# Moving the conditions' set-up of a fused MoE, linear-attention and local-attention kernel

## The chip, the cores and the metric

The kernel runs on one core of a Trainium2 chip. The metric is the device time of one execution in microseconds (us), here the median of three runs. One more execution was recorded by the hardware profiler; all times inside the kernel are from that one, counted from the start of its span. All data are 32-bit floats.

## The reference

The input `x` is 4 batches of 512 rows of 256 numbers, with a condition of 64 numbers for each batch. Three parts follow each other:

```
x = x + linear_attention(mixture_of_experts(x, cond))
x = x + ffn_and_local_attention(conditioned_attention(x, cond))
```

The mixture has 8 experts of three layers (256 to 512 to 512 to 256) and takes two of them for each row. The linear attention has 8 heads in blocks of 32 rows. The conditioned attention has 16 heads, and mixes its softmax with a "field" over the positions that depends on the condition alone. That field is what this case is about:

```
fp = layernorm(relu(cond @ We1.T + be1) @ We2.T + be2, ln_g, ln_b)   # 4 x 256
fa = softmax(fp @ pe.T)                                               # 4 x 512, pe: sines of the positions
mod = (1 - 0.21) * mod + 0.21 * fa                                    # in the conditioned attention
```

The condition also gives a bias to the conditioned attention's coherence (`cond` times a part of `Wc1`, plus `bc1`). Last come two layers of a local attention with a gated feed-forward.

## The kernel before

**Experts.** The rows are sorted by expert into slots of 256 or 128 rows. `SLOTS` lists 24 of them; the last two (`rare`) run only if the routing needs them, under a run-time branch (`tc.If`, L1508). For each of the others (`often`), the loop at L1487 does the first layer (`layer`, matmuls into `ph`, then the activations `h`, by turns on ACT and DVE), then the third layer of the slot before (`last`: matmuls into `po`, a bias addition on DVE into `ob`, L1464, and one indirect DMA of 128 rows on POOL's queue into the table `ys` in DRAM, L1469, one or two of them), then the second layer. The last of these slots has 128 rows, the one before it 256. The scatters all write `ys`, and each waits until the one before has landed. In iterations 2 and later one weight of the later stages is loaded each (`later`), so the weights of the conditions are there some iterations before the loop ends.

**The conditions' set-up.** `conditions` (L229) is a generator of small operations on 4 or 8 columns, with two `yield`s, so three parts:

- first: `pcs` (the condition times two weights), `csb` and `hdT` on DVE, `pfp`, and the layer norm of `fp` on DVE, with a square root on ACT (L250);
- second: two transposes of `fp` (`pfpT`), a copy, `pfs` (the product with the positions, 512 wide), and a copy of it into `fa` (L264);
- third: maximum `fmx` (L267), Exp with its sum `fsum` on ACT (L269), scaling, four transposes (`pfaT`) and a copy into `faT`.

Before, the first part stands behind the loop and ahead of the branch, the second behind the branch, and the third is chained into the linear attention's work for the first batch (`fill`, L1681), from which pieces are taken between the steps of the attention. `faT` and `csb` are used in the conditioned attention, more than 100 us later.

**Filling.** `busy(n)` (L1390) puts n matmuls 512 wide whose result nobody reads (`pbusy`) into PE's queue. It reads batch 0's `xres`, so POOL's addition to it (L1557) waits for the last of them.

**Results.** `results(b)` (L1521) loads batch b's two rows of `ys` for each row into `g0` and `g1`, two buffers of each; batch 0's in halves, the second row's on ACT's queue, all others on SP's. `weighted(b)` (L1532) scales them on ACT (`g`, L1535) and adds on DVE (`ymoe`, L1536). Batches 2 and 3 get the buffers of batches 0 and 1. The linear attention's `front` then transposes `ymoe` (`pt`), copies it (`yT`), and multiplies (`pqk`, `pv`); `features` does `pf` and, on ACT, `ex`.

**What sets the order.** A planner puts the instructions of each engine into its queue: of those that it takes to be ready, the one earliest in the program goes first. So work can run ahead of its place in the program, or behind it. Instructions pinned to program order (those under `PE.in_order()`, `busy` and the whole linear attention on PE among them) keep behind whatever the program issued before them on the engine. The matmuls of the experts' layers and of `conditions` are not pinned where it is called from the experts' stage. On the chip each queue runs in order.

The calls around the branch, before:

```
            last(len(often) - 1, often[-1])
            aside = conditions(cw_, wp)
            next(aside)
            busy(1)
            with tc.If(halves > NHALF - NRARE):
                ...
            busy(3)
            next(aside)
            busy(1)
```

Of the kernel before, what the change touches and what calls it, by code (L numbers as in the profile page):

```python
# [12 lines left out]
F32 = mybir.dt.float32  # L13
I32 = mybir.dt.int32
AF = mybir.ActivationFunctionType
ALU = mybir.AluOpType
AX = mybir.AxisListType
PSUM = bass.MemoryType.PSUM

B, S, H = 4, 512, 256  # L20
# [43 lines left out]
def adaln_attn_ffn_kernel(ctx: ExitStack, tc: tile.TileContext, a: dict, out: bass.AP):  # L64
    nc = tc.nc
# [40 lines left out]
    def bank(kind, name):  # L106
        return ps_now["pool"].tile([128, 512], F32, tag=kind, name=name, bufs=ps_now[kind])

    def mmt(name):
        return bank("mm", name)  # L110

    def tpt(name):
        return bank("tp" if "tp" in ps_now else "mm", name)

    def acct(name):
        return bank("acc" if "acc" in ps_now else "mm", name)
# [10 lines left out]
    def mm(dst, pairs):  # L127
        for i, (lhsT, rhs) in enumerate(pairs):
            PE.matmul(dst, lhsT, rhs, start=(i == 0), stop=(i == len(pairs) - 1))
# [11 lines left out]
    def run(pieces):  # L141
        for _ in pieces:
            pass
# [22 lines left out]
    def col(name, i=0):  # L166
        at = COLS[name][0] + i
        return cols[:, at : at + 1]
# [11 lines left out]
    def row(name):  # L180
        return rows[name]
# [49 lines left out]
    def conditions(W, cp):  # L231

        csb = cp.tile([128, 2, B], F32, tag="csb", name="csb", bufs=1)
        hdT = cp.tile([128, 2, B], F32, tag="hdT", name="hdT", bufs=1)
        for c in range(2):
            ps = acct("pcs")
            PE.matmul(ps[:, 0:B], W["wc1c"][:, c * 128 : (c + 1) * 128], W["csT"], start=True, stop=True)
            PE.matmul(ps[:, B : 2 * B], W["we1"][:, c * 128 : (c + 1) * 128], W["csT"], start=True, stop=True)
            nc.vector.tensor_scalar(csb[:, c, :], ps[:, 0:B], col("bc1", c), None, ALU.add)
            nc.vector.tensor_scalar(hdT[:, c, :], ps[:, B : 2 * B], col("be1", c), 0.0, ALU.add, ALU.max)  # L240
        ps = acct("pfp")
        mm(ps[:B, :H], [(hdT[:, c, :], W["we2"][:, c, :]) for c in range(2)])
        fp = cp.tile([B, H], F32, tag="fp", name="fp", bufs=1)
        nc.vector.tensor_tensor(fp, ps[:B, :H], row("be2")[:B, :], ALU.add)
        st = cp.tile([B, 6], F32, tag="fst", name="fst", bufs=1)
        nc.vector.bn_stats(st, fp)
        mv = cp.tile([B, 2], F32, tag="fmv", name="fmv", bufs=1)
        nc.vector.bn_aggr(mv, st)
        rs = cp.tile([B, 1], F32, tag="frs", name="frs", bufs=1)
        nc.scalar.activation(rs, mv[:, 1:2], AF.Sqrt, bias=eps5[:B, :])  # L250
        nc.vector.reciprocal(rs, rs)
        nc.vector.tensor_scalar(fp, fp, mv[:, 0:1], rs, ALU.subtract, ALU.mult)
        nc.vector.tensor_tensor(fp, fp, row("lng")[:B, :], ALU.mult)
        nc.vector.tensor_tensor(fp, fp, row("lnb")[:B, :], ALU.add)
        yield
        pt = tpt("pfpT")
        for c in range(2):
            PE.transpose(pt[:, c * B : (c + 1) * B], fp[:, c * 128 : (c + 1) * 128], ident[:B, :B])
        fpT = cp.tile([128, 2, B], F32, tag="fpT", name="fpT", bufs=1)
        nc.vector.tensor_copy(fpT, pt[:, : 2 * B].rearrange("p (c b) -> p c b", b=B))  # L260
        ps = mmt("pfs")
        mm(ps[:B, :], [(fpT[:, c, :], W["peT"][:, c, :]) for c in range(2)])
        fa = cp.tile([B, S], F32, tag="fa", name="fa", bufs=1)
        nc.vector.tensor_copy(fa, ps[:B, :])  # L264
        yield
        fmx = cp.tile([B, 1], F32, tag="fmx", name="fmx", bufs=1)
        nc.vector.reduce_max(fmx, fa, axis=AX.X, negate=True)  # L267
        fsum = cp.tile([B, 1], F32, tag="fsum", name="fsum", bufs=1)
        nc.scalar.activation(fa, fa, AF.Exp, bias=fmx, accum_out=fsum)  # L269
        nc.vector.reciprocal(fsum, fsum)  # L270
        nc.vector.tensor_scalar(fa, fa, fsum, FIELD, ALU.mult, ALU.mult)
        pt = tpt("pfaT")
        for t in range(NT):
            PE.transpose(pt[:, t * B : (t + 1) * B], fa[:, t * 128 : (t + 1) * 128], ident[:B, :B])
        faT = cp.tile([128, NT, B], F32, tag="faT", name="faT", bufs=1)
        nc.vector.tensor_copy(faT, pt[:, : NT * B].rearrange("p (t b) -> p t b", b=B))
        W["csb"], W["faT"] = csb, faT
# [865 lines left out]
    with ExitStack() as abc:  # L1143
        wp = abc.enter_context(tc.tile_pool(name="wp", bufs=1, reuse_waits="tile"))
# [6 lines left out]
        with ExitStack() as moe:  # L1151
# [35 lines left out]
            with PE.in_order():  # L1187
# [7 lines left out]
                for n, b in enumerate((0, 2, 3, 1)):  # L1195
# [6 lines left out]
                    for t in range(NT):  # L1202
                        nc.scalar.activation(sq[:, t, :], xres[b][:, t, :], AF.Square,
                                             accum_out=ss[:, b * NT + t : b * NT + t + 1])
# [45 lines left out]
            rest = xp.tile(G, F32, tag="rest", name="rest")  # L1250
# [139 lines left out]
            def busy(n):  # L1390
                with PE.in_order():
                    ps = mmt("pbusy")
                    for _ in range(n):
                        PE.matmul(ps, ident, xres[0].rearrange("p t h -> p (t h)")[:, :512], start=True, stop=True)
# [86 lines left out]
            cw_ = {}  # L1481
# [3 lines left out]
            gather(0, ds[0])  # L1485
            often, rare = ds[:-NRARE], range(len(ds) - NRARE, len(ds))
            for j, d in enumerate(often):  # L1487
                if j == len(often) - 2:
                    halves = nc.values_load(nhalf[0:1, 0:1], min_val=0, max_val=2 * NE)
                if j == 1:  # L1490
                    weights()
                h1 = layer(d, d.xbT, "h1", d.w1[:, 8:].rearrange("p (c m) -> p c m", m=ME), 0)
                if j:
                    last(j - 1, ds[j - 1])
                if j + 1 < len(often):
                    loads(j + 1, ds[j + 1])
                    gather(j + 1, ds[j + 1])
                    if j > 1 and later:
                        name, behind[0] = next(iter(later)), True
                        cw_[name] = later.pop(name)()  # L1500
                        behind[0] = False
                d.h2 = layer(d, h1, "h2", d.w2, 4)
            last(len(often) - 1, often[-1])

            aside = conditions(cw_, wp)
            next(aside)
            busy(1)
            with tc.If(halves > NHALF - NRARE):  # L1508
                for j in rare:
# [3 lines left out]
                    h1 = layer(d, d.xbT, "h1", d.w1[:, 8:].rearrange("p (c m) -> p c m", m=ME), 0)  # L1513
                    d.h2 = layer(d, h1, "h2", d.w2, 4)
                    last(j, d)
            busy(3)
            next(aside)
            busy(1)


            def results(b):  # L1521
# [21 lines left out]
        with ExitStack() as lin:  # L1543
# [111 lines left out]
            def beside(b):  # L1655
                if b + 1 < B:
                    nxt = front(b + 1, ds[b + 1])
                else:
                    nxt = cond_front(cw_, 0, cond_first, False, v1s, wp, gp, {"xT2": "g0", "cT": "g1"})
                for _ in range(6):  # L1660
                    next(nxt, None)
                    yield
                if b > 0:
                    yield from tail(b - 1, ds[b - 1])
                yield from nxt

            with PE.in_order():


                rest = front(0, ds[0])  # L1670
                for _ in range(4):
                    next(rest)
                features(ds[0], 0)
                for _ in range(2):
                    next(rest)
                fill = iter(())
                for k in range(len(steps) + 1):
                    b, u = steps[k] if k < len(steps) else (B, 0)
                    if u == 0:
                        run(fill)  # L1680
                        fill = (beside(b) if b else chain(rest, aside, beside(0))) if b < B else iter(())  # L1681
                    if b < B:
                        ds[b].fm_now = ds[b].fm
                    if u % 2 == 0 and k > 0:
                        b0, u0 = steps[k - 1]
                        values(ds[b0], u0 // 2)
                        next(fill, None)
                    if k + 1 < len(steps):
                        b1, u1 = steps[k + 1]
                        features(ds[b1], u1)  # L1690
                    next(fill, None)
                    if b < B:
                        scores(ds[b], u)
                    next(fill, None)
                run(fill)
# [3 lines left out]
        with ExitStack() as cst:  # L1699
# [3 lines left out]
            cp = cst.enter_context(tc.tile_pool(name="cp", bufs=2, reuse_waits="tile"))  # L1703
# [10 lines left out]
    with ExitStack() as again:  # L1714
        again.enter_context(banks("ps3", mm=4, tp=2, acc=2))
        with tc.If(wrong > 0):
            with ExitStack() as cst:
                wp = cst.enter_context(tc.tile_pool(name="wp2", bufs=1))
                cp = cst.enter_context(tc.tile_pool(name="cp2", bufs=2))
# [130 lines left out]
```

## Time and profile before

| what | value |
|---|---|
| median of three runs | 1389.45 us (1389.37 to 1392.45) |
| profiled execution, its time | 1390.6 us |
| profiled execution, its span | 1388.8 us |
| mean granted clock of TensorE | 0.988 |
| PE busy | 1336.5 us (96%), 7624 matmuls |
| DVE busy | 655.3 us (47%) |
| ACT busy | 587.2 us (42%) |
| POOL busy | 233.2 us (17%) |
| PE's share of the chain that ended last | 88% |

The span runs from the first to the last instruction; the execution's own time has 1.8 us more. PE is TensorE's matmul row, PEld its weight loads, DVE the vector engine, ACT the scalar engine, POOL GpSimd, SP the engine that issues most DMAs. A float32 matmul shows as two rows of each. The granted clock is the share of full speed at which TensorE was let run in a stretch. The releaser of a wait is inferred from semaphore events.

### The profile page before, as it was taken

The page shows a single profiled execution, that of the slowest core. Times are in us where ns is not written, and L with a number is a line of the kernel's source. Part 1 is how long each engine was busy: PE and PEld are TensorE (multiplying, and loading weights), DVE is VectorE, ACT ScalarE, POOL GpSimd, SP SyncE. Part 2 cuts the span into 40 slices and gives each one's busy share as a digit, 9 for nine tenths or more (in the row PEclk, how much of TensorE's full clock was granted, in tenths as well). Part 3 has the DMA queues.
Part 4 walks back from the last instruction along what each step waited for, and adds up shares of the span by engine and source line. Part 5 has one row for each costly group of instructions (what it writes and reads, how often), then busy time and mean ns, then how long its engine had stood idle before and what let it go on. Part 6 is the DMA issues. An engine that isn't in the chain of part 4 may idle for free.

```text
span 1388.8 us, 19451 instructions
## 1 busy us (share of the span) xinstructions
PE 1336.5 (96%) x7624; PEld 828.0 (60%) x7624; DVE 655.3 (47%) x1296; ACT 587.2 (42%) x997; POOL 233.2 (17%) x223
## 2 busy tenths in 40 slices
PE   5999999998999999999999999999999999999998
PEld 4788888883666633333335555656655556556654
DVE  6122222225777633332227697654362767864421
ACT  4111111115555355454655746662223657474111
POOL 1324322211000011010103232100020322310110
PEclk8999999999999999999999999999999999999999
DMA  4577667633000000000201001210001010011000
GB/s 142 208 255 261 234 217 251 203 131 125 1 2 1 1 0 1 1 1 1 88 30 43 17 25 32 77 41 24 23 0 42 24 33 24 17 40 40 23 24 25
DMA packets 43085, 94.74 MB, mean 68 GB/s; under 512 B 9568, under 2 KB 25064, under 8 KB 40168
## 3 DMA queue, kind: packets, MB, share of 16 engines
q1 hardware_dynamic: 37560, 81.81, 17.7%
q0 software_dynamic: 3792, 10.24, 2.2%
q8 instruction: 63, 1.03, 0.3%
q10 hardware_dynamic: 1632, 1.34, 0.3%
q14 instruction: 38, 0.31, 0.1%
HBM read 84.08 MB, written 7.21 MB: 66 GB/s over the span
## 4 chain that ended last, share of the span: by engine, by line
PE 88%; DVE 6%; ACT 2%; DMA 2%; issue 1%; POOLq 0%; POOL 0%; DVEq 0%; SPq 0%; ACTq 0%
PE ph L78 14%; PE pdq L78 12%; PE pfy L78 6%; PE pug L78 5%; PE pv L78 5%; PE pua L78 5%; PE sc L78 5%; PE po L78 4%; PE pn L78 4%; PE pdy L78 4%; PE pds L78 4%; PE pz L78 2%; PE pqt L82 2%; PE pcy L78 1%; PE pck L78 1%
## 5 line engine op out<-in xcount | busy, mean ns | idle before, releaser
L78 PE MATMUL pdq<-wqkv,yT 128*128 128x512 f32 x384 | 177.1, 602 | 0.0
L419 ACT ACTIVATE cex<-sc 128x1024 f32<-128x1024 f32 x128 | 124.0, 1021 | 99.7 <-PE sc L78 99.0
L78 PE MATMUL ph<-h,w 128*128 128x256 f32 (+1 forms) x704 | 132.9, 346 | 0.4 <-DVE h L1403 0.4
L627 POOL TENSOR_TENSOR qr<-t,t 128x512 f32<-128x512 f32 x64 | 85.9, 1342 | 266.5 <-DVE t L624 229.3
L671 DVE TENSOR_TENSOR p<-p,lmask 128x384 f32<-128x384 f32 (+1 forms) x128 | 92.2, 734 | 69.4 <-ACT p L669 68.2
L78 PEld LDWEIGHTS ph<-h,w 128*128 128x128 f32 x704 | 116.2, 191 | 12.6 <-DVE h L1403 0.8
L78 PEld LDWEIGHTS pdq<-wqkv,yT 128*128 128x128 f32 x384 | 69.6, 190 | 78.1 <-issue 72.8
L1401 ACT ACTIVATE h<-ph,w 128x256 f32<-128x256 f32 (+1 forms) x88 | 35.3, 437 | 190.1 <-PE ph L78 132.2
L1403 DVE TENSOR_SCALAR h<-ph,w 128x256 f32<-128x256 f32 (+1 forms) x88 | 36.1, 438 | 165.7 <-PE ph L78 102.1
L669 ACT ACTIVATE p<-pds,ss 128x256 f32<-128x256 f32 (+1 forms) x256 | 95.8, 456 | 38.8 <-PE pds L78 30.3
L78 PE MATMUL pug<-hT,w 128*128 128x512 f32 x160 | 76.8, 602 | 0.0
L78 PE MATMUL sc<-qm,kT 32*128 32x512 f32 x512 | 76.2, 647 | 0.3 <-ACT cex L419 0.3
L78 PE MATMUL pua<-hT,w 128*128 128x512 f32 x160 | 75.2, 592 | 0.0
L617 ACT ACTIVATE sq<-pdq 128x512 f32<-128x512 f32 x64 | 38.3, 598 | 85.8 <-PE pdq L78 48.1
L78 PE MATMUL pv<-cex,v 128*32 128x512 f32 x512 | 69.1, 605 | 3.6 <-DVE xT L293 2.1
L78 PE MATMUL ph<-xbT,w 128*128 128x256 f32 (+1 forms) x352 | 69.1, 349 | 0.5 <-ACT xbT L123 0.5
L390 POOL TENSOR_SCALAR fterm<-vw,faT 128x256 f32<-128x256 f32 x16 | 14.6, 921 | 323.4 <-DVE cr L380 323.4
L78 PE MATMUL po<-w,h 128*128 128x256 f32 x296 | 67.6, 379 | 0.5 <-ACT h L1401 0.5
L78 PE MATMUL pds<-qT,kT 64*128 64x256 f32 (+1 forms) x512 | 65.3, 375 | 0.0
L78 PEld LDWEIGHTS pds<-qT,kT 64*128 64x128 f32 x512 | 43.9, 186 | 32.9 <-issue 24.7
L78 PEld LDWEIGHTS ph<-xbT,w 128*128 128x128 f32 x352 | 59.2, 193 | 6.8 <-ACT xbT L123 0.7
L78 PE MATMUL pdy<-wo,oT 128*128 128x256 f32 x256 | 61.5, 386 | 0.0
(302 smaller groups left out, 2131.5 us busy)
## 6 DMA issues: line engine op xcount, KB each, us to landing
w<-in_moe_w_dram SPq DMA_DIRECT2D x22, 1024.0 KB
w<-in_moe_w_dram SPq DMA_DIRECT2D x22, 640.0 KB
w<-in_moe_w_dram SPq DMA_DIRECT2D x22, 516.0 KB
zb<-rows SPq DMA_DIRECT2D x32, 256.0 KB
g<-ys SPq DMA_DIRECT2D x6, 512.0 KB
wqkv<-in_f_wqkv_dram SPq DMA_DIRECT2D x2, 1536.0 KB
w<-in_f_w_dram SPq DMA_DIRECT2D x2, 1408.0 KB
out_dram<-yc SPq DMA_DIRECT2D x16, 128.0 KB
```

Of the source, the lines that this page charges most:

```text
L78: cls._queue(nc.tensor.matmul(*args, **kw))
L82: cls._queue(nc.tensor.transpose(*args, **kw))
L390: nc.gpsimd.tensor_scalar_mul(fterm[:, t, :], vw, W["faT"][:, t, b : b + 1])
L419: nc.scalar.activation(ex, pss[j], AF.Exp, scale=CHD**-0.5)
L617: nc.scalar.activation(sq, p3, AF.Square)
L627: nc.gpsimd.tensor_tensor(qr_t[:, s], t1, t2, ALU.add)
L669: nc.scalar.activation(p[:, at], pss[r][:, at], AF.Exp, scale=d.ss[:, 2 * u + jj, 1, 2 * c + r : 2 * c + r + 1])
L671: nc.vector.tensor_tensor(p[:, :n], p[:, :n], lmask[:, :n], ALU.mult)
L1401: nc.scalar.activation(dst, src, AF.Relu, bias=bias)
L1403: nc.vector.tensor_scalar(dst, src, bias, 0.0, ALU.add, ALU.max)
```

## The change

The first part of `conditions` is called at the head of the loop's last iteration, ahead of that slot's first layer. The second part is called behind the loop, ahead of the branch; the copy of `pfs` into `fa` is dropped, and the maximum and Exp read `pfs` in PSUM. The third part is split by a new place of the second `yield`: maximum, Exp and scaling come directly behind the branch, then `busy(4)`, then the transposes and `faT`, then `busy(2)`. Before it was `busy(3)`, the second part, `busy(1)`. The chain into the linear attention no longer holds a part of it.

```diff
@@ conditions
         ps = mmt("pfs")
         mm(ps[:B, :], [(fpT[:, c, :], W["peT"][:, c, :]) for c in range(2)])
-        fa = cp.tile([B, S], F32, tag="fa", name="fa", bufs=1)
-        nc.vector.tensor_copy(fa, ps[:B, :])
         yield
         fmx = cp.tile([B, 1], F32, tag="fmx", name="fmx", bufs=1)
-        nc.vector.reduce_max(fmx, fa, axis=AX.X, negate=True)
+        nc.vector.reduce_max(fmx, ps[:B, :], axis=AX.X, negate=True)
+        fa = cp.tile([B, S], F32, tag="fa", name="fa", bufs=1)
         fsum = cp.tile([B, 1], F32, tag="fsum", name="fsum", bufs=1)
-        nc.scalar.activation(fa, fa, AF.Exp, bias=fmx, accum_out=fsum)
+        nc.scalar.activation(fa, ps[:B, :], AF.Exp, bias=fmx, accum_out=fsum)
         nc.vector.reciprocal(fsum, fsum)
         nc.vector.tensor_scalar(fa, fa, fsum, FIELD, ALU.mult, ALU.mult)
+        yield
         pt = tpt("pfaT")
@@ the experts' loop
             for j, d in enumerate(often):
+                if j == len(often) - 1:
+                    aside = conditions(cw_, wp)
+                    next(aside)
                 if j == len(often) - 2:
@@ behind the loop
             last(len(often) - 1, often[-1])
-            aside = conditions(cw_, wp)
             next(aside)
             busy(1)
             with tc.If(halves > NHALF - NRARE):
...
-            busy(3)
             next(aside)
-            busy(1)
+            busy(4)
+            run(aside)
+            busy(2)
@@ the linear attention
-                        fill = (beside(b) if b else chain(rest, aside, beside(0))) if b < B else iter(())
+                        fill = (beside(b) if b else chain(rest, beside(0))) if b < B else iter(())
```

## The prediction

> **What bounds the kernel now.** The page first: PE is busy for 96% of the span and carries 88% of the chain that ended last. So the change, which touches some 45 us out of 1388.8, is worth what it takes from or adds to the start of the dense PE work behind it. I then read the chain of waits from 250 us on (before 304 us it is matmuls alone), the instructions in order of time from 296 to 358 us, and stretches with the granted clock.
>
> The chain of waits, in order of time (start, us, what):
> ```profile
> 304.51 0.70 DVE ob L1464
> ...
> 305.48 3.84 DMA ys<-ob,goal
> ...
> 309.58 2.53 DMA ys<-ob,goal
> ...
> 312.86 3.15 DMA ys<-ob,goal
> ...
> 316.07 3.18 DMA g<-ys
> ...
> 320.52 3.46 PE pfs L78 x4
> 323.98 1.07 PE pbusy L78 x2
> ...
> 328.99 3.82 DMA g<-ys
> ...
> 332.89 0.91 ACT g L1535 x2
> ```
> Between experts and attention PE waits for transfers. The last-but-one slot's result (`ob`, 304.51) starts three scatters, each held until the one before has landed: 305.48, 309.58, 312.86, all landed at 316.0. Batch 0's rows are then loaded and weighted; its last `ymoe` ends at 322.04 (two of 0.44 from 321.16). PE is not free then: it does `pfs` and a `pbusy`, and the first transposes of the attention (`pt`) start at 325.09, 3.05 late. Further on, batch 3's loads start when batch 1's last `ymoe` ends (328.96) and land at 332.81, with ACT waiting for them ahead of the features.
>
> Instructions in order of time (start, us, engine, line; in brackets the idle time before and its releaser):
> ```profile
> 308.56 1.99 PE L78 MATMUL po<-w,h 128*128 128x256 f32 x8 [0.52 <-ACT h L1401]
> 311.60 1.11 PE L78 MATMUL pfp<-cwe,hdT 128*4 128x256 f32 x4
> 315.04 2.81 PE L78 MATMUL pbusy<-xres,ident 128*128 128x512 f32 x6 [1.27 <-DVEq L1508]
> 316.62 1.28 ACT L250 ACT_TABLE_LOAD   x1 [7.33 <-DMA ys<-ob,goal]
> 325.09 1.09 PE L82 MATMUL pt<-ident,ymoe 128*128 128x128 f32 x8
> 326.43 1.28 ACT L269 ACT_TABLE_LOAD   x1
> ```
> The Sqrt of the set-up comes before the branch in the program, yet ran behind ACT's wait for the scatters. Queue order is thus the planner's, and it can differ from the program's.
>
> Stretches (length, then busy us of PE, PEld, DVE, ACT, POOL, granted clock, DMA share, GB/s):
> ```profile
> 295.00:300.00 5.00, 5.00 (x29) 4.51 (x28) 0.73 (x2) 0.84 (x2) 0.97 (x1) 1.00 0.35 140
> 320.50:324.00 3.50, 3.48 (x5) 0.46 (x5) 1.15 (x3) 2.34 (x6) 0.00 (x0) 0.54 0.98 336
> 342.00:346.00 4.00, 4.00 (x22) 3.51 (x22) 1.90 (x3) 1.57 (x2) 0.00 (x0) 0.72 0.00 0
> ```
> PE has no free time among the experts, and `pfs` ran at about half clock.
>
> **First part, moved ahead of the last slot's first layer.** Its weights were there long before 310 us and no gap took its matmuls, so I put them where the program now has them: behind the last-but-one slot's second layer (about 299.0), ahead of `po` of that slot. Eight `pcs` matmuls take 1.05 (310.48 to 311.60 less the wait of 0.09), four `pfp` 1.04 (311.60 to 312.64). PE is full, so `po`, `ob` and the first scatter move by 2.1: 305.48 becomes 307.6. The scatters keep their spacing (4.10, 3.28, 3.14) and all have landed at 318.1. Bounds: nothing, if PE finds a gap such as the 0.52 at 308 or the matmuls come behind `po`; 2.5, if PE also waits for `hdT`, where its weight load stood 0.42. I take 2.1.
>
> DVE's share is 1.85 up to the variance, 1.37 behind the root (0.15, 0.40, 0.41, 0.41); ACT's is 1.28 table load and 0.29. From 301 on the chain ends near 306.2, before `ob` is due at 306.6. Queued behind the Sqrt on ACT are the last slot's first-layer `h`. They must be done when PE ends `po` (306.5); the Sqrt ends near 304.7, and the four take 1.6. Free, then, with 0.2 in hand; an overrun reaches only the third scatter, which has 1.9 of room (`ob` of the last slot would be ready at 313.1, its turn is 315.0).
>
> **Second part, directly behind the experts.** `pfpT` 0.25, copy 0.16, `pfs` four at 0.43 at full clock (as `pbusy`, six in 2.81) instead of 3.46. About 312.7 to 315.2, wholly inside the wait for the scatters, so nothing on the path. `busy(1)` ends near 316.0; the branch then takes what it took, 1.27, and `busy(4)` runs to about 320.7.
>
> **Third part.** The copy of `fa` (0.68) goes. The maximum now reads PSUM: 0.67 from SBUF, 0.69 for a 512-wide PSUM copy, so no change. Exp needs its table: 1.28 + 0.72 + 0.19. I put it behind ACT's two load issues, where the Sqrt was: 318.9 to 321.1. Batch 0's rows land at 321.3 (3.18 after their issue), so the weighting on ACT is not held, by 0.2. The last transposes (0.7) and `busy(2)` (0.86 each) follow until about 324.0.
>
> A rule that speaks against this: the Trainium skill (ScalarE: Activation LUTs, What ACT_TABLE_LOAD costs) puts a switch of table set at some 2.66 us, a load of 1283 ns and a drain as long again. Here Sqrt starts at 317.92, 0.02 behind its load's end: the load agrees, the drain is not there. By the page Exp would end at 322.5 and the sum below would be +0.6; by the row it is what follows.
>
> **The sum.** `pt` now waits for `ymoe` alone: 322.04 + 2.1 = 324.14 instead of 325.09, a gain of 0.95. But everything that hangs on the loads is 2.1 later. Batch 1's data, there at about 323.6 (some 2.1 MB moved by then, at 336 to 354 GB/s in the stretches), come at 325.7. Its four `ymoe` (0.47 each) no longer queue behind the copy and the maximum, but one of them still meets POOL's `xres` addition (one took 1.73 instead of 0.47). They end between 327.6 and 329.0; I take 328.4, against 328.96. Batch 3's loads and ACT's chain behind them come 0.6 earlier. That is the later bound, so it decides: -0.6. Four transposes (0.7) leave PE at 348.4, but there the chain goes from `pf` to ACT's `ex` at 349.05, which they do not hold: nothing, bound -0.7. The profiled execution took 1390.6 (span 1388.8 and 1.8 around it), which gives 1390.0. Its time is 1.15 above the median of the runs, so in their terms 1389.45 - 0.6 = 1388.8. By the bounds (first part 0 to 2.5, `ymoe` 327.6 to 329.0, transposes, the clock at 342) the forecast's own range is -3.2 to +2.
>
> **Rivals.** *ACT's queue comes free as well.* If the first part's matmuls cost PE nothing ahead of `po` (-2.1) and the planner no longer puts batch 3's weighting ahead of the features, whose wait at 332.89 was 2.22, the gain is 0.6 + 2.1 + 2.2 = 4.9: 1384.5. For it: DVE and ACT lose some 2 us each of work in 324 to 330. Against it: PE is 5.00 busy in each 5 us from 250 to 305.
>
> *The softmax ahead of ACT's loads* (slower). If Exp comes first in ACT's queue, it waits for the maximum (about 318.0) and ends at 318.9, and ACT's half of batch 0's loads starts 0.8 late, behind SP's batch 1 (1 MB, 3 us at 353 GB/s). Batch 0 is weighted up to 3 later, `pt` starts at 327.1, and batch 3's loads land at 334.4, +1.6. PE would then stand for 3 us. Before, a gap of 2.0 (317.85 to 319.87) was followed by 0.54; a cold run costs some 1.9 (the first `pv` 3.61, the second 1.73), so up to +3.5, and with the wait of 0.4 for `hdT` +3.9: 1393.3. It decides from an Exp that starts later than 317.2. For it: program order. Against it: where the Sqrt ran.
>
> The Trainium skill (TensorE: Matmul & The Clock Gate, What's actually happening) has the half clock after an idle window of about 3.4 us. The trace shows it after 2.0, so the shorter gap decides here.
>
> *No effect:* the 3 us that PE gets back are paid by the scatters' 2.1 and the loads; it is the forecast's upper half.
>
> **How the numbers follow.** Forecast 0.52, free queue 0.25, softmax ahead of the loads 0.18, other orders of the replanned queues 0.05 (either sign; an extra wait of 1.2 in each of the four batches of about 35.5 us would be +4.8). A measurement of this kernel tells about 0.3%, 4.2 us, from no change. Faster by more: most of the free queue and the forecast's lowest end, 0.27. Slower by more: the upper half of the softmax case, with a stall on ACT or another order on top, 0.2. Same 0.53. The range takes the free queue's 1384.5 with a little more gain and the softmax case's upper end: 1384.2 to 1393.6.
>
> **What would show it.** Right: `pcs` near 299; first scatter near 307.6, the last landed near 318.1; `pfs` in about 1.9 at clock 1.0 before the branch; Exp behind ACT's loads; `pt` near 324.1; batch 3's loads landing near 332.2. Wrong: the first scatter still at 305.5, Exp ahead of the loads, a half clock over `pt` and `pqk`, or `g` of batch 3 elsewhere on ACT.

## The result, and the profile after

The changed kernel took 1386.4 us (median of 9 runs, 1382.35 to 1387.08), the kernel before 1389.53 beside it (9 runs): a ratio of 0.997, 95% interval 0.9959 to 0.998. In a second series, the run `again` below, it was 1383.66 against 1387.28, ratio 0.9977 (0.9968 to 0.9986). Every ratio in this document is to the kernel before, run beside it in the same series. So the change saves 3 to 4 us, about 0.3%, where the forecast was 0.6. The profiled execution of after took 1386.8, span 1385.0, against 1390.6 and 1388.8 before: 3.8 less.

The chain of waits of the changed kernel (start, us, what), for the lines shown of before:

```profile
310.75 1.02 PE pfs L78 x2
311.78 1.94 PE po L78 x8
313.74 0.44 DVE ob L1464
...
314.44 3.15 DMA ys<-ob,goal
...
318.09 4.42 DMA g<-ys
...
323.08 1.97 DVE ymoe L1539 x2
...
326.43 5.36 PE pqk L78 x8
...
333.81 0.50 ACT g L1538
334.31 0.94 ACT ex L1599
...
339.94 1.92 PE pv L78 x8
```

The long `pfs` with its `pbusy` ahead of the attention (320.52 before) is gone from the chain; half of `pfs` is now on it further up, ahead of the last slot's `po`. Batch 3's loads (328.99 before) are gone too: behind `pqk` the chain goes on with the features, and ACT's `g` of batch 3 (333.81) stands between two `ex` with no wait for data.

Instructions of the changed kernel in order of time (start, us, engine, line; in brackets the idle time before and its releaser):

```profile
301.81 1.03 PE L78 MATMUL pfp<-cwe,hdT 128*4 128x256 f32 x4
...
304.52 1.28 ACT L250 ACT_TABLE_LOAD   x1
...
315.40 0.68 ACT L268 ACTIVATE fa<-pfs,fmx 4x512 f32<-4x512 f32 x1 [2.57 <-DVE fmx L265]
...
322.31 2.34 POOL L1560 TENSOR_TENSOR xres<-xres,crows 128x1024 f32<-128x1024 f32 x1 [5.20 <-DMA g<-ys]
...
323.08 2.25 DVE L1539 SCALAR_TENSOR_TENSOR ymoe<-g,m,g 128x256 f32<-128x256 f32 x2 [0.55 <-ACT g L1538]
...
324.99 1.16 PE L82 MATMUL pt<-ident,ymoe 128*128 128x128 f32 x6 [2.16 <-DVE ymoe L1539]
...
332.89 1.02 ACT L1598 ACTIVATE ex<-pf 128x1024 f32<-128x1024 f32 x1 [1.00 <-PE pf L78]
...
333.81 0.50 ACT L1538 ACTIVATE g<-g,m 128x256 f32<-128x256 f32 x1
```

The first part lies among the last slot's matmuls, and Exp (315.40) lies ahead of the loads, not behind them. POOL's addition to `xres` now runs beside batch 0's last two `ymoe`: 2.25 for the two, against 0.88 for the same two before (321.16). ACT's `g` of batch 3 (333.81) comes behind the first `ex`, where before two of them came ahead of it and had waited 2.22 for their loads.

Stretches of the changed kernel (length, then busy us of PE, PEld, DVE, ACT, POOL, granted clock, DMA share, GB/s):

```profile
312.50:315.50 3.00, 3.00 (x10) 1.11 (x8) 1.10 (x2) 0.43 (x2) 0.97 (x1) 1.00 0.03 5
...
326.00:330.00 4.00, 3.72 (x7) 1.60 (x6) 2.27 (x5) 1.29 (x3) 0.00 (x0) 0.57 0.83 263
...
480.00:484.00 4.00, 4.00 (x64) 3.07 (x66) 2.05 (x6) 0.05 (x1) 1.93 (x3) 0.58 0.00 0
```

and one of the kernel before:

```profile
490.00:494.00 4.00, 3.93 (x20) 1.39 (x20) 0.01 (x1) 0.93 (x2) 2.29 (x3) 0.62 0.00 0
```

`pfs` runs at full clock now. But half clock stands elsewhere: over `pqk` at 326 and over the matmuls at 480 in after; over the first `pv` at 342 and over the conditioned attention at 490 in before.

To see where the time went, both traces are counted from the same place, the transposes `pxb` of the last slot's input rows (291.94 before, 291.85 after), which stand ahead of everything that was moved. All times in the experiments below that are called "from pxb" are counted so. Some names of the linear attention's later steps are needed: `psc` are the score matmuls behind the features, `pn` and `pz` the numerator and denominator in PSUM, `z` the reciprocal of the denominator, and `aT` their product on DVE.

| event, us from pxb | before | after | difference |
|---|---|---|---|
| first scatter of the last-but-one slot | 13.54 | 15.87 | +2.33 |
| batch 0's loads issued | 24.13 | 25.80 | +1.67 |
| first `pt` | 33.15 | 30.25 | -2.90 |
| last `pt` done | 34.24 | 34.30 | +0.06 |
| first `pqk` (its 8 took 3.70, 5.36) | 34.53 | 34.58 | +0.05 |
| first `ex` | 41.76 | 41.04 | -0.72 |
| first `pv` (3.68, 1.99) | 48.82 | 48.03 | -0.79 |
| first `psc` | 52.33 | 49.86 | -2.47 |
| reciprocal `z` at the linear stage's end | 194.10 | 193.26 | -0.84 |
| first `pv` of the conditioned attention | 198.13 | 195.71 | -2.42 |
| end of the span | 1096.86 | 1093.15 | -3.71 |

The clock's part behind the start of `pqk` can be taken out, as an estimate. Half clock cost before 1.69 (`pv`, 3.68 instead of 1.99) and 1.42 (from the conditioned attention's first `pv` to its second 4.07 instead of 2.65), together 3.11; after 1.66 (`pqk`, 5.36 instead of 3.70) and 1.63 (`psc` to `z`: the whole difference between the kernels there is put down to the half clock at 480), together 3.29. So the clock gave nothing there (+0.18), and the work is 3.89 shorter: 2.44 up to `psc` (2.47 + 1.66 - 1.69), by that count nothing from there to `z`, 1.58 from `z` to the conditioned `pv`, and 0.13 back later. The half clock over `pfs` (3.46 before, for two times 1.02 after) lies ahead of `pqk`, and nothing of it is left there: `pqk` starts at the same time in both. The experiments ask for the cause of the 2.44 and the 1.58, and for what became of the 0.95 that PE was to gain and the 2.1 that it was to pay.

### The profile page after: what moved, and what is told of

It reads as the page before. It is cut to its first block, busy times and chain, and to the rows that moved or that the text cites. A ratio compares the mean times of both kernels' runs of the same rounds, so it can differ in the third digit from the quotient of the medians.

```text
span 1385.0 us, 19458 instructions
## 1 busy us (share of the span) xinstructions
PE 1338.2 (97%) x7628; PEld 829.6 (60%) x7628; DVE 655.0 (47%) x1295; ACT 587.7 (42%) x997; POOL 232.7 (17%) x223
## 4 chain that ended last, share of the span: by engine, by line
PE 89%; DVE 5%; ACT 2%; DMA 1%; issue 1%; SPq 0%; POOLq 0%; POOL 0%; DVEq 0%
PE ph L78 14%; PE pdq L78 12%; PE pfy L78 6%; PE pug L78 5%; PE pv L78 5%; PE pua L78 5%; PE sc L78 5%; PE po L78 5%; PE pn L78 4%; PE pdy L78 4%; PE pds L78 4%; PE pz L78 2%; PE pqt L82 2%; PE pqk L78 1%; PE pcy L78 1%
## 5 line engine op out<-in xcount | busy, mean ns | idle before, releaser
L390 POOL TENSOR_SCALAR fterm<-vw,faT 128x256 f32<-128x256 f32 x16 | 14.6, 925 | 323.0 <-DVE cr L380 323.0
L78 PEld LDWEIGHTS pds<-qT,kT 64*128 64x128 f32 x512 | 43.9, 186 | 32.9 <-issue 25.0
```

The lines of the kernel that those rows point to most:

```text
L78: cls._queue(nc.tensor.matmul(*args, **kw))
L390: nc.gpsimd.tensor_scalar_mul(fterm[:, t, :], vw, W["faT"][:, t, b : b + 1])
```

## The experiments

**The 1.58 at the linear stage's end.** Before, the conditioned attention's first `pv` waits for the last `aT`:

```profile
490.07 1.08 PE L78 MATMUL pv<-cex,v 128*32 128x512 f32 x8 [1.50 <-DVE aT L1633]
```

and after it does not:

```profile
487.56 1.07 PE L78 MATMUL pv<-cex,v 128*32 128x512 f32 x8
```

That `pv` reads nothing of `aT`. But `aT` reads `pn` in PSUM, and a new tile in the bank of `pn` has to wait for it. The third part's `pfaT` took a bank of the linear stage's four before, and takes none there after. The theory: this moves `pn` to another bank. The rival: it is the matmuls that left. `again` is the changed kernel once more; `bank1` gives back one bank with four tiny transposes in `pfaT`'s old place, `bank4` takes four banks with sixteen:

```diff
+            def spare():
+                for _ in range(1):          # bank4: range(4)
+                    pt = tpt("pspare")
+                    for t in range(NT):
+                        PE.transpose(pt[:, t * B : (t + 1) * B], ident[:B, :], ident[:B, :B])
+                return
+                yield
-... chain(rest, beside(0)) ...
+... chain(rest, spare(), beside(0)) ...
```

> The changed kernel once more, as the base of the other runs on this chip. Both theories: 3 to 4 us below the kernel before (ratio 0.997). The start of the linear attention and the place of the half-clock stretches are looked at: if the 1.7 us that the first pv gained (1.92 instead of 3.61) is the clock's phase, it can be gone in this profile; if it follows from the order of the work, pv takes about 1.9 again and pqk about 5.4.

> The changed kernel with four 4-column transposes of the identity into one bank of their own, whose result nobody reads, at the place in the linear attention where pfaT was. Theory A (the later half of the gain is that pfaT no longer takes one of the linear attention's four PSUM banks, so the banks come in another order at the end of the stage): the first pv of the conditioned attention waits for aT again, about 1.5 us, and the time is 1.2 to 1.8 us above the changed kernel (ratio to the kernel before about 0.998). Theory B (PE's work that left the stage, 0.4 to 0.7 us of transposes): at most 0.7 us above the changed kernel, seen at 346 to 350 us, and no wait of pv for aT.

> The same with four banks and sixteen transposes, four times the work, but four banks are a whole turn. Theory A: no wait of the first pv for aT, the time within 0.7 us of the changed kernel (ratio about 0.9975). Theory B: four times the loss of the run with one bank, 1.6 to 2.8 us above the changed kernel.

Measured: `again` 1383.66, ratio 0.9977 (0.9968 to 0.9986); `bank1` 1386.16, 0.9989 (0.998 to 0.9999); `bank4` 1383.12, 0.9971 (0.9957 to 0.9985). From `z` to the first `pv`: 2.45, 4.03, 2.44. In `bank1` the wait is back, to the hundredth:

```profile
484.56 1.06 PE L78 MATMUL pv<-cex,v 128*32 128x512 f32 x8 [1.50 <-DVE aT L1636]
```

`bank4`, with four times the extra matmuls, has none. So it is the bank. One caution: the profiled spans of `bank1` and `again` are equal (1380.5 and 1380.9), as the execution of `again` had half clock at 323 to 326 and at 538 to 541 and that of `bank1` nowhere between 280 and 700. The medians are 2.5 apart, but the intervals of the two ratios overlap, so it is the traces that decide here.

From the other side, the same with three spare banks was tried in the kernel before, so that with `pfaT` four are taken:

```diff
-... chain(rest, aside, beside(0)) ...
+... chain(rest, aside, spare(), beside(0)) ...     # spare with range(3)
```

> The kernel before with 12 transposes of 128x4 more (about 0.7 us of PE in all), into three spare banks behind pfaT in the linear stage. With pfaT's own that makes four, a full turn of the four banks, so the banks stand at the stage's end as in the changed kernel. Theory (the turn of the banks is what the 1.58 us at the linear stage's end come from): the conditioned attention's first pv no longer waits for the last aT; from the reciprocal z to pv 2.45 instead of 4.03; 1 to 1.6 us less in all, ratio 0.9985 to 0.9995. Rival (it needs the changed set-up): pv still waits 1.50, ratio 1.0 to 1.001.

1387.74, ratio 1.0 (0.9992 to 1.0009), and the wait of 1.50 is still there. The expectation failed, and the banks in the built programs show why: they fit a rule by which a tile gets the bank that was given back first, not the next in a fixed turn. The tile behind the stage's first ten gets bank 6 in every kernel: `pfaT` before, `pt` after. In `bank4` the four spares, which nobody reads, take 6, 5, 4, 7 and give them back in that order, so `pt` has 6 as in after. In `before_bank3` they take 5, 4 and 7 behind `pfaT`, but `pfaT`'s own bank is given back later, by the copy that reads it, and `pt` gets 5 as before. So no bank behind them moved, and nothing was tested but this.

What can be read off each program is the bank itself. The conditioned `pv` is in bank 6 everywhere. The last `pn` is in bank 6 in before, `bank1`, `before_bank3`, `before_gpin` and `before_gpin3`, and all five wait 1.50 or 1.51; it is in bank 7 in after and in the eight other kernels, and none of them waits. That settles the place; only the count of four is dropped.

**The 0.95 of PE.** `busy` reads `xres`, so POOL's addition waits for the last `pbusy`. If that is why the last `ymoe` were slow, `busy` off another tile should free them:

```diff
+            warm = [xres[0].rearrange("p t h -> p (t h)")[:, :512]]
             def busy(n):
...
-                        PE.matmul(ps, ident, xres[0].rearrange("p t h -> p (t h)")[:, :512], start=True, stop=True)
+                        PE.matmul(ps, ident, warm[0], start=True, stop=True)
...
+            warm[0] = cw_["peT"][:, 0, :]
             next(aside)
```

> The changed kernel with the filling matmuls behind the experts reading the positions' table instead of batch 0's xres, so that POOL's addition to xres need not wait for the last of them. If that addition, which ran at 322.3 to 324.7 beside batch 0's ymoe, is what ate PE's gain: ymoe of batch 0 takes 4 x 0.47 without a stall, its last one ends near 323.7 instead of 325.4, pt and pqk come 1.4 to 1.7 us earlier, PE stands less and keeps its clock; 1.5 to 3 us below the changed kernel (ratio about 0.9955). Rival (the loads set the pace there): ymoe's end and pqk move by less than 0.4, and the time does not change.

1383.28, ratio 0.997 (0.9959 to 0.9981). The two `ymoe` took 0.88, and `pt` was done 32.56 from pxb instead of 34.30. So the collision with POOL is what ate the gain at `pt`. The time that was expected of it, 1.5 to 3 us, did not come: `again` took 1383.66 on the same chip. `pqk` started at 34.17, only 0.41 sooner:

```profile
324.40 3.70 PE L78 MATMUL pqk<-yT,awqkv 128*128 128x512 f32 x8 [1.61 <-ACT yT L123]
```

ACT's half of the copy `yT` stood behind three weightings of batch 1 that waited for their loads. The next step takes that copy off ACT:

```diff
-                    evac(yT[:, c, :], pt)
+                    (evac if b else nc.vector.tensor_copy)(yT[:, c, :], pt)
```

> The change, with busy reading the positions' tile instead of xres (as in busyother, so that POOL's addition runs early) and batch 0's two yT copies both on DVE, so that neither stands behind ACT's weighting of batch 1. In busyother the pt were done 1.74 earlier, but pqk only 0.4. Theory (ACT's yT copy behind three weightings held pqk): pqk at 32.9 to 33.5 behind the pxb transposes, 1.2 to 1.7 earlier than in the changed kernel, ex at most that much earlier than busyother's 38.98, ratio 0.9955 to 0.997. Rival (DVE's own queue, with batch 1's ymoe in it, takes as long): pqk at 34 or later, ratio as busyother's 0.997.

1382.41 against 1388.5, ratio 0.9952 (0.9939 to 0.9965): below the interval of `again`, and the best of all. `pqk` started 32.82 from pxb, 1.76 sooner than after:

```profile
321.45 1.16 PE L82 MATMUL pt<-ident,ymoe 128*128 128x128 f32 x6 [0.64 <-DVE ymoe L1542]
...
322.96 3.70 PE L78 MATMUL pqk<-yT,awqkv 128*128 128x512 f32 x8 [0.35 <-DVE yT L1570]
```

The theory's number came to within 0.1 (32.9 to 33.5 expected). Against `busyother` the two cannot be told apart: the intervals overlap, `ex` is at 38.66 and 38.98, and `psc` in `best3` at 48.39 instead of 47.80, after half clock over its second `pqk` (4.81 instead of 3.70).

**The 2.1 of the first part.** `first_behind` calls the first part behind the loop again, right ahead of the second. `pfs_pinned` calls it behind `po` of the last-but-one slot, and holds the second part in program order on PE, so that `pfs` can't slip ahead of the last `po`:

```diff
# first_behind
-                if j == len(often) - 1:
-                    aside = conditions(cw_, wp)
-                    next(aside)
...
+            aside = conditions(cw_, wp)
+            next(aside)
             next(aside)
# pfs_pinned: the three lines stand behind last(j - 1, ...) in the loop, and
-            next(aside)
+            with PE.in_order():
+                next(aside)
```

> The change with its first part alone undone: pcs, pfp and the Sqrt stand behind the last slot again, directly ahead of the second part. If the first part's 2.0 us of PE ahead of po are what the loads are late by (the theory), the first scatter starts 2.0 earlier against the pxb transposes of the last slot (13.5 to 14 us behind them instead of 15.9), the third no longer waits for half of pfs, and batch 0's loads start near 24.1 to 24.5 instead of 25.8; pqk then comes 1 to 1.7 earlier. If the first part was free and the scatters' own spacing sets the loads, they stay at 25.8. Rival: the root, which now follows pcs on ACT, brings fmx and Exp behind the branch and into ACT's load issues or the weighting, which gives the gain back. Theory: ratio to the kernel before 0.996 to 0.9975; rival 0.998 to 1.0.

> The change, with the first part called behind po of the last-but-one slot instead of ahead of it, and the second part's instructions on PE held in the order of the program, so that pfs stays behind the last slot's po. Theory (PE's 2.0 us ahead of po, and half of pfs ahead of the last po, are what made the scatters late): first scatter back at 13.5 to 14 us behind the pxb transposes, third near 20.9 to 21.5, batch 0's loads near 24.2 to 24.9, pqk up to 1 earlier if nothing else holds it. Rival (what holds pqk is POOL's addition beside batch 0's ymoe): loads earlier, pqk the same within 0.3 or later. Ratio 0.996 to 0.998 by both, so the profile decides.

`first_behind`: 1387.19, ratio 0.9995 (0.9987 to 1.0004). The theory's scatter and loads came, and the rival's time. The first scatter was back at 13.54 and the loads at 24.41, 1.39 sooner than after: the first part is not free. But the `pqk` that was to come 1 to 1.7 sooner came 3.93 later (38.51), and the gain was given back:

```profile
314.58 17.79 SPq L1530 DMA_DIRECT2D g<-ys  x8
...
315.35 0.37 PE L82 MATMUL pfpT<-ident,fp 4*128 4x4 f32 x2 [4.41 <-DVE fp L254]
...
315.98 3.57 PE L78 MATMUL pfs<-peT,fpT 128*4 128x512 f32 x4 [0.26 <-DVE fpT L260]
...
320.31 0.68 ACT L268 ACTIVATE fa<-pfs,fmx 4x512 f32<-4x512 f32 x1 [5.29 <-DVE fmx L265]
...
321.27 0.91 ACTq L1530 DMA_DIRECT2D g<-ys  x2
```

The layer norm starts behind the experts, PE waits 4.41 for it, `pfs` runs at half clock, and Exp, which stands ahead of ACT's loads, holds them until 321.27, 6.7 behind SP's. The first `pt` came at 37.19 from pxb, against 30.25.

`pfs_pinned`: 1385.37, ratio 0.9981 (0.9973 to 0.999). The first scatter was back at 13.53, but the third could not start before 22.47, as in after (22.59), since `ob` of the last slot was no sooner (311.70, 21.77 from pxb; in after 21.89, in before 18.65):

```profile
307.40 1.28 ACT L250 ACT_TABLE_LOAD   x1 [7.15 <-DVE fmv L248]
...
309.29 2.37 PE L78 MATMUL po<-w,h 128*128 128x256 f32 x8 [0.65 <-ACT h L1401]
```

Against before, that `ob` is 3.24 later in after: 2.33 by the first part, as at the first scatter, and the other 0.91 by the half of `pfs` ahead of `po`. In `pfs_pinned` it is 3.12 later: 2.61 by the first part, and 0.51 because the Sqrt on ACT and the rest of the layer norm on DVE now stand among the last slot's second-layer `h`, so that `po` waits 0.65 and takes 2.37, where before it waited 0.52 and took 1.99. So the pin took `pfs` away and the new place put nearly as much back. That scatter then took 4.45 to land, not 3.15, and the loads came later than in after: 26.98. The theory's 24.2 to 24.9 failed. PE is full among the experts, so over 2 us are paid for the first part wherever it is put ahead of the last `po`: ahead of the first scatter or of the last. Why a scatter takes 2.7 in one kernel and 4.5 in another stays open.

Is it ACT's late load issue that makes `first_behind` slow? `behind_sp` gives those loads to SP:

```diff
-                        queue = nc.scalar if b == 0 and k == 1 else nc.sync
+                        queue = nc.sync
```

> first_behind with one thing more: batch 0's loads all issue from SP, none from ACT. In first_behind ACT issued its half 6.7 us behind SP's (321.27 against 314.58), since fmx and Exp stood ahead of it, and the attention's pt began 37.2 us behind the pxb transposes of the last slot. Theory (Exp ahead of ACT's load issues is what made first_behind slow): loads again near 24.4, pt begins 28.5 to 31.5, pqk 31 to 34, ratio 0.9955 to 0.998. Rival (the late pfs at half clock and the pbusy runs hold PE, or ACT's weighting still stands behind Exp): pt begins at 34 or later, ratio 0.9985 or more.

Ratio 0.9977 (0.9968 to 0.9986). The rival held for `pt`: 37.22, no sooner. PE's queue shows what holds it:

```profile
315.78 0.37 PE L82 MATMUL pfpT<-ident,fp 4*128 4x4 f32 x2 [4.34 <-DVE fp L254]
316.41 3.57 PE L78 MATMUL pfs<-peT,fpT 128*4 128x512 f32 x4 [0.26 <-DVE fpT L260]
319.92 1.92 PE L78 MATMUL pbusy<-xres,ident 128*128 128x512 f32 x2
322.13 3.67 PE L78 MATMUL pbusy<-xres,ident 128*128 128x512 f32 x8 [0.30 <-ACT g L1537]
325.73 0.41 PE L82 MATMUL pfaT<-ident,fa 4*128 4x4 f32 x4
326.07 1.98 PE L78 MATMUL pbusy<-xres,ident 128*128 128x512 f32 x4
327.89 1.04 PE L82 MATMUL pt<-ident,ymoe 128*128 128x128 f32 x8
```

ACT's four weightings of batch 0, behind Exp, are done at 323.34. But DVE's copy `faT` stands ahead of the last three `ymoe` and waits 3.52 for `pfaT`, which is behind `busy(4)`; and `pt` stands behind `busy(2)`. So what is late here is the set-up on PE, which waits 4.34 for the layer norm and then runs at half clock until 321.5, with the fillers in their fixed place behind it; for Exp and the branch behind it PE is idle for only 0.30. No run leaves the fillers out, so this is read from the trace and not tested. The theory's time (0.9955 to 0.998) did come, further on: `psc` came 3.15 sooner than in `first_behind`, 1.3 of it by the clock over `pv`, and ACT, which in `first_behind` waits 1.35 and 1.17 for later batches' loads around its first `ex`, waits for none.

`best4` puts `best3`'s two edits on `behind_sp`:

> behind_sp with best3's two edits: the first part directly ahead of the second behind the last slot, batch 0's loads all on SP, busy off xres, batch 0's yT copies on DVE. If the 1.4 us that the loads gain by the first part's later place carry through once Exp is out of their way: loads near 24.4, pqk 1 to 1.5 earlier than in best3, ratio 0.9945 to 0.9965. If pfs at half clock and Exp then hold PE or ACT instead: pqk no earlier than in best3, ratio 0.997 or more.

1386.41, ratio 0.9985 (0.9976 to 0.9994): the loads at 23.65, the soonest of all, and `pqk` at 38.11, 5.3 later than in `best3`. The rival again: PE's queue is the same, with `pt` directly behind `busy(2)`, and DVE's `faT` waits 3.02 for `pfaT`. Sooner loads are worth nothing behind a late set-up; this is what the first part's early place buys for its 2 us.

**The 2.44 ahead of `psc`.** The theory: batch 3's two weightings, with their wait of 2.22, stood ahead of `ex` on ACT before, and do not after. `before_gpin` holds ACT's weighting of batches 1 to 3 in program order in the kernel before, `before_gpin3` that of batch 3 alone:

```diff
-                    nc.scalar.mul(gs[0][:, t, :], gs[0][:, t, :], tops[0][:, i : i + 1])
+                    scaled = nc.scalar.mul(gs[0][:, t, :], gs[0][:, t, :], tops[0][:, i : i + 1])
+                    if b == 3:              # before_gpin: if b:
+                        tc.keep_in_program_order(scaled)
```

> The kernel before, with ACT's weighting muls of batches 1 to 3 held in the order of the program, so that batch 3's two no longer stand ahead of the features' ex. Theory (they and their wait of 2.22 for batch 3's loads cost the kernel before its last 0.9 us ahead of ex): ex starts 0.9 to 1.5 earlier against the pxb transposes (41.76 in the kernel before). Rival (ex was held by pf on PE, and the difference of 0.72 between the kernels is from elsewhere): ex stays within 0.3. The time: 0 to 1.5 us less, unless the weighting of the later batches, now later, holds a later step; ratio 0.9985 to 1.001.

> The kernel before with ACT's weighting of batch 3 alone held in the order of the program. before_gpin (batches 1 to 3) brought ex 3.7 and the first psc 6.0 earlier against the pxb transposes, but lost 14.6 between psc and z. Theory (batch 3's two weightings ahead of ex cost the kernel before both the late ex and, through PE's idle time, the half-clock first pv): ex near 38 to 40, the first pv in about 1.99 instead of 3.68, psc near 46.4 to 48.5; the loss behind it is batch 3's own, a third of before_gpin's or less, 0 to 5. Rival (batch 1's or 2's order did it): ex stays within 0.5 of 41.8 and pv at 3.3 to 3.8. Ratio 0.996 to 1.0 by the theory, 0.999 to 1.003 by the rival.

`before_gpin`: 1395.15, ratio 1.0053 (1.004 to 1.0066), slower than expected. `ex` came at 38.05 from pxb, 3.7 sooner than before, more than the 0.9 to 1.5 expected, and `psc` at 46.36, 6.0 sooner; but from `psc` to `z` it took 156.4 instead of 141.8. It moved batch 1's weighting too, and `pqk` came 1.29 sooner, so it does not show batch 3's part alone. `before_gpin3`: 1390.4, ratio 1.0014 (1.0005 to 1.0023). `ex` at 39.47, 2.29 sooner, `pv` in 1.99, `psc` at 47.79, 4.54 sooner, of which 1.69 is the clock; from `psc` to `z` 148.5, a loss of 6.7 where 0 to 5 was expected, and so the time lay in the rival's range and not in the theory's. Lines of `before_gpin3`, in order of time:

```profile
329.97 1.02 ACT L1597 ACTIVATE ex<-pf 128x1024 f32<-128x1024 f32 x1 [0.60 <-PE pf L78]
...
404.67 3.35 DVE L1634 RECIPROCAL z<-z 128x512 f32<-128x512 f32 x1 [2.15 <-ACT z L1629]
...
408.47 0.30 PE L82 MATMUL pt<-ident,ymoe 128*128 128x128 f32 x1 [4.56 <-DVE ymoe L1538]
```

With nothing ahead of it, `ex` waits for `pf` alone; so the two weightings cost the kernel before 2.3 at `ex` and 2.85 at `psc`, and the theory holds for these two steps, close to the 2.44. The price of moving them to their place in the program is shown as well: batch 3's `ymoe` then stand on DVE behind a `z` of 3.35, PE waits 4.56, and half clock follows (granted clock 0.5 from 410 to 416). In the changed kernel they are between the two, among the `ex` of the first batch, and nobody waits for them. Which part of the change put them there was not tested by itself, but in all ten kernels whose third part has left the attention, `first_behind` too, the first `ex` goes ahead of batch 3's weighting, and in before and `before_bank3` it goes behind two of its pieces.

## Why the prediction was right, and where its sizes were not

It said same or a little faster, 0.6, in a range down to 1384.2; 1386.4 lies inside, but 3 to 4 is not 0.6. That it lies inside is in part luck: the range reached so far down for a rival half of which came true, and 1.58 of the gain has a cause that the prediction did not name. Step by step:

- **First part ahead of `po`, 2.1.** Right in place and nearly in size: `pcs` at 299.07, first scatter at 307.72 (307.6 said), 2.33 later from pxb. "The scatters keep their spacing" was wrong: the second came 2.83 behind the first instead of 4.10, and the third waited for `ob` (313.74), in part because two of the four `pfs` matmuls ran ahead of the last `po`. The two errors nearly cancelled, and the loads came 1.67 later from pxb, not 2.1. The Sqrt cost nothing, but not for the reason given: ACT's first-layer `h` (303.35 and 304.13) ran ahead of it (table load at 304.52), not behind.
- **Second part hidden, at full clock.** Half right: full clock, but half of it ahead of the last `po`, 1.0 on the chain, 0.91 of it a delay.
- **Exp behind ACT's loads.** Wrong: Exp ran at 315.40, before the branch. It cost nothing, since that is before the 317.2 from which the rival of the softmax ahead of the loads was to decide. `first_behind` has that order with a late maximum (319.59), and its ratio is 0.9995 against 0.9977 of the change; part of that is the loads behind Exp (`behind_sp`, without them, is back at 0.9977, some of it by the clock), but its late `pt` is put down to PE's queue.
- **`pt` sooner by 0.95.** Mis-sized. PE did come free (first `pt` 2.90 sooner), but the last `ymoe` met POOL's addition and `pt` ended 0.06 later. The prediction knew the addition and its price (1.73 instead of 0.47), and let it meet batch 1's `ymoe`, not batch 0's; that `busy` reads `xres`, and so sets when the addition starts, was not followed through.
- **"That is the later bound, so it decides: -0.6."** This is the step that failed. Batch 1's last `ymoe` ended at 328.45 (328.4 said), but batch 3's data came about 333.3 (the DMA share falls from 1.04 to 0.26 behind 333), not at 332.2, as batch 2's were still moving (DMA share 0.83 from 326 to 330, where before it had been 0.15). And nobody waited: batch 3's weighting had gone behind `ex`. That was one half of the rival called ACT's queue comes free, priced at 2.2; the runs put it at 2.4 (`before_gpin3` 2.3 to 2.85). Its other half, a free first part, was wrong. The two should not have been tied into one case.
- **Four transposes leave the linear stage: nothing, bound -0.7.** Mis-sized, and for a reason that was not looked for: with `pfaT`'s bank gone, `pn` lies elsewhere and a wait of 1.50 in another stage, 150 us later, falls away (1.58 from `z` to `pv`).
- **The clock.** Half clock over `pqk` was named as a sign of error. It came, and cost about what was saved by its absence elsewhere (3.29 against 3.11).

## What to carry to other kernels

When instructions leave one engine's queue, look at what the planner will let move up or down in that queue: here the transfer that was late stayed late, and the gain was that the wait for it went behind work that was ready. A tile that leaves a rotating pool can change which bank every later tile gets; the first tile of the next stage is where to look for a wait on a reader it has nothing to do with. And a filler instruction is a reader like any other: what it reads decides which later writer it holds up, and its fixed place in the queue decides what stands behind it when the work ahead of it is late (`behind_sp`).

## What the runs showed of the hardware that was not expected

Half clock (granted clock 0.50) comes, away from both ends of the span, in stretches of 3.41 us or a multiple of it, and where PE is full a stretch of 3.41 costs 1.4 to 1.7 us. Within one execution the starts lie a whole number of 3.41 us apart: in before 320.32, 340.80, 490.98 and 719.68, which is 6, 44 and 67 steps. The place differs between executions of the same kernel (after: from 326.4, 480.0 and 715.5; `again`: from 323.0 and 538.1). The gap just ahead does not decide alone: before has a stretch from 491 on, behind a wait of 1.50, and `bank1` has none behind the same wait; in after the one at 480 follows waits of 0.42 and 0.41. The Trainium skill (TensorE: Matmul & The Clock Gate, What's actually happening) has the half clock after an idle window of about 3.4 us. The length of the stretches agrees. The idle time does not: in the 3.41 us ahead of these stretches of before and after PE was idle for 0.83 to 2.32 us, never for all of it, and here the measurement decides; what counts as idle stays open. For reading results: two single profiles of kernels that differ by a wait of about 1.5 us can show the same span, and did (`bank1` and `again`).

A 128x1024 addition on POOL (2.34) beside two `ymoe` on DVE stretched them from 0.88 to 2.25, in a place where neither touches the other's data. Nearly all of it fell on the first of the two, which took 1.85 and ended 0.28 behind the addition's end (324.65).
